# A coarse column shift inside the score matmul, coefficients shared between VectorE and GpSimd, and gates in two F32R passes

## The chip, the cores and the metric

The kernel runs on 1 core of a Trainium2 chip. The metric is device microseconds of one execution; a run of the kernel before takes 1344.95 us in the median of three (1344.68 to 1345.1). PE is TensorE, DVE is VectorE, ACT is ScalarE, POOL is GpSimd, and SP is the engine whose queue issues most of the DMAs.

## The reference

One transformer layer on x of 16 batches, 512 positions and 128 features: an attention and a feed-forward network (FFN), each on a layer-normed input, each layer-normed again and added. A head has 8 features (16 heads), a query is its own key, and every position has one of 64 buckets per head.

```python
scores = jnp.einsum('bhsd,bhtd->bhst', q, q) / jnp.sqrt(jnp.float32(E))
same = (b_hs[:, :, :, None] == b_hs[:, :, None, :]).astype(scores.dtype)
attn = jax.nn.softmax(scores * (NB - 2 + same), axis=-1)      # NB = 64
...
h = silu(tlin(x, w1_w, w1_s)) * tlin(x, w2_w, w2_s)           # tlin: x @ w.T * s, w of -1, 0, 1
h = gelu(tlin(h, h1_w, h1_s)); h = gelu(tlin(h, h2_w, h2_s))  # 512 wide
return tlin(h, w3_w, w3_s)
```

Scores times 62 or 63 make large exponents, so something has to be subtracted ahead of the exponential. All is in fp32.

## The kernel before

The program is straight-line code. A small planner (class Order) builds it: the parts of the work are generators that ask for an engine with a cost, a rank and what they wait for, and the planner's own clock decides the order in which each engine gets its instructions. On the chip every engine runs its list in that order. Buffers are named and handed out by pools (`logit_bufs`, `score_banks`, `ffn_banks`, `banks` and so on). Lower rank goes first: score matmuls have 0, attention 1, FFN 4.

*Batch preparation* (`prep`). The layer norm of x is applied by ACT with statistics that ACT sums ahead of time (`inputs`, L553 and L563). PE projects the queries (L635), which are split into three bf16 parts and written to DRAM. Buckets come from PE and go to DRAM too.

*Scores* (`gather`, `scores`). For each of 256 heads SP loads the parts back as 72 rows for the left and 72 for the right operand, nine products of parts and 8 features; one bf16 matmul of 128 x 512 per tile (L872), four tiles a head. A third load puts the head's bucket row on all partitions (bb).

*Coefficients* (`coeffs`, L890). DVE compares bb, kept as three rows of 172, with the bucket of the partition and adds 62.

*Logits* (`logits`, L925). DVE multiplies coefficient and score and keeps the row maximum of the tile. Scores are symmetric, so row maxima are column maxima.

*Shift and exponential* (`maxima`, `softmax`). Two heads' maxima are transposed by DVE (L958), written to DRAM (md), read back as one row on all partitions (mb, 256 KB), and POOL subtracts it from four tiles at once (L982). ACT takes the exponential (L987). Five heads of the first two batches go another way (`softmax_by_rows`).

*Weighted sum* (`attend`). For each group of four heads PE multiplies with the values (L1048); the result is copied, transposed, and divided by DVE (L1079, L1080). A logit buffer is held from its first tile to the group's product; there are 11.

*FFN* (`residual`, `added`, `ffn`). After the norms, PE makes the w1 and w2 gates in fp32 (L1200, eight matmuls a batch), ACT silu, DVE the product (L1170); two hidden layers (L1244, gelu L1258), and the output (L1282). The mean is taken out in the weights, not in the input. The FFN of batch b waits for the first hidden layer of batch b - 1; batch 15 goes in halves. POOL has the power -0.5 of the variances (L457). Dummy matmuls (`activity`, L1419) fill PE until the first FFN.

Of the kernel before, what the change touches and what calls it, by code (L numbers as in the profile page):

```python
# [14 lines left out]
BF16 = mybir.dt.bfloat16  # L15
AF = mybir.ActivationFunctionType
# [5 lines left out]
P = 128  # L22
EPS = 1e-5
NBKT = 64

# [165 lines left out]
def tile_lsh_attention_ffn(  # L191
    ctx: ExitStack,
    tc: tile.TileContext,
    x: bass.AP,
# [30 lines left out]
    KS = NP * NP * DH  # L225
    BR, BC, BP = 3, 172, 174
# [9 lines left out]
    LB = 11  # L236
    BY_ROWS = (3, 7, 11, 15, 19)
    SLOTS = H * NT
    N = B * SLOTS

# [39 lines left out]

    junk = const.tile([P, E], BF16, name="junk")
# [7 lines left out]

    block = const.tile([E, H], F32, name="block")  # L290
    nc.vector.reduce_sum(
        block, ident.rearrange("r (h d) -> r h d", d=DH), axis=AX.X
    )
    hp_sb = const.tile([E, H, NH], F32, name="hp_sb")
# [68 lines left out]
    score_banks = Pool("s", 3)  # L363
    ffn_banks = Pool("f", 3)
    banks = Pool("b", 2)
    logit_bufs = Pool("l", LB)
    row_bufs = Pool("r", 4)
    co_bufs = Pool("co", 4)
    mx_bufs = Pool("mx", 2)
    mb_bufs = Pool("mb", 3)  # L370
    row_mx_bufs = Pool("rx", 2)
    h_bufs = Pool("h", 3)
    x1_bufs = Pool("x1_", 2)
    xnt_bufs = Pool("xntf", 1)
    avs_bufs = Pool("avs", 1)
    a_bufs = Pool("a", 2)

    NB_ = B * NG
    gathered, exped = events(B * H), events(B * H)
    scored, weighed = events(N), events(N)  # L380
# [116 lines left out]
    def turned(xn, xnt, k, tp, tiles):  # L497

        cols = slice(tiles[0] * P, (tiles[-1] + 1) * P)

        def turn():
            for t in tiles:
                nc.tensor.transpose(tp[:, ts(t, P)], xn[:, t, :], ident)

        yield pe(0.125 * len(tiles), 2, turn)
        yield act(0.13 + 0.0925 * len(tiles), -2, lambda: nc.scalar.copy(xnt[:, cols], tp[:, cols]))
        od.put(banks, k)
# [21 lines left out]
    rs_x = const.tile([P, B, NT], F32, name="rs_x")  # L529
    nm_x = const.tile([P, B, NT], F32, name="nm_x")  # L530
    known = events(B)

    def inputs():
        for b0, b1 in zip(GROUPS, GROUPS[1:]):
            n = b1 - b0
            sums = const.tile([P, 2, n, NT], F32, name=f"sx_{b0}")
            ve = const.tile([P, n, NT], F32, name=f"vx_{b0}")
            late = 6 if b0 == 1 else LATE
            if b0 > 1:
                yield wait(gathered[1])  # L540
            for b in range(b0, b1):
                xt = p2.tile([P, NT, E], F32, tag="xtm", name=f"xtm_{b}", bufs=1)
                yield dma(
                    256,
                    2,
                    lambda: nc.sync.dma_start(
                        out=xt, in_=x[b].rearrange("(p t) e -> p t e", t=NT)
                    ),
                )

                def sum_(ts_):
                    for t in ts_:
                        nc.scalar.activation(  # L553
                            junk,
                            xt[:, t, :],
                            AF.Identity,
                            scale=ROOT / E,
                            accum_out=sums[:, 0, b - b0, t : t + 1],
                        )

                def square(ts_):
                    for t in ts_:
                        nc.scalar.activation(  # L563
                            junk,
                            xt[:, t, :],
                            AF.Square,
                            scale=-ROOT,
                            bias=sums[:, 0, b - b0, t : t + 1],
                            accum_out=sums[:, 1, b - b0, t : t + 1],
                        )  # L570

                yield act(1.0, late, lambda: sum_((0, 1)))
                yield act(1.0, late, lambda: sum_((2, 3)))
                yield act(1.2, late, lambda: square((0, 1)))
                yield act(1.2, late, lambda: square((2, 3)))
            yield act(
                0.22,
                -5,
                lambda: nc.scalar.activation(ve, sums[:, 1], AF.Identity, bias=eps),
            )  # L580
            yield pool(
                1.0,
                0,
                lambda: nc.gpsimd.tensor_tensor(
                    rs_x[:, b0:b1], ve, mhalf[:, 0:n], op=ALU.pow
                ),
            )
            k = yield get(banks)
            mp = bank(k, f"mp_{b0}")[:, 0 : n * NT].rearrange("p (b t) -> p b t", t=NT)
            yield act(0.22, -5, lambda: nc.scalar.copy(mp, sums[:, 0]))  # L590
            yield dve(
                0.1,
                1,
                lambda: nc.vector.scalar_tensor_tensor(
                    nm_x[:, b0:b1], mp, -(float(E) ** 0.5), rs_x[:, b0:b1], op0=ALU.mult, op1=ALU.mult
                ),
            )
            od.put(banks, k)
            for b in range(b0, b1):
                od.set(known[b])  # L600


    qds, bkds, bjs = {}, {}, {}

    def prep(b):
# [14 lines left out]
        if b:  # L620
            yield wait(known[b])
            xn = p2.tile([P, NT, E], F32, tag="xna", name=f"xn_a{b}", bufs=1)
            xnt = p1.tile([P, S], F32, tag="xnta", name=f"xnt_a{b}")
            yield from rescale(xt, lambda t: xn[:, t, :], (nm_x[:, b], rs_x[:, b]), ALL)
            k = yield get(banks)
            yield from turned(xn, xnt, k, bank(k, f"tp_a{b}"), ALL)
        else:
            xnt = p1.tile([P, S], F32, tag="xnta", name=f"xnt_a{b}")
            yield from norm_transposed(xt, xnt, f"a{b}", 1, ALL)
# [13 lines left out]
        qd = [  # L643
            dram.tile([H, DH, NP, S], BF16, tag="qd0", name=f"qd0_{b}"),
            dram.tile([H, NP, DH, S], BF16, tag="qd1", name=f"qd1_{b}"),
        ]
        kept = events(NP)

        def keep(i):
            def emit():  # L650
                nc.sync.dma_start(out=qd[0][:, :, i, :], in_=qparts[i])
                nc.sync.dma_start(out=qd[1][:, i, :, :], in_=qparts[i])

            yield dma(256, 1, emit, cost=0.7)
            od.set(kept[i])
# [97 lines left out]
        od.spawn(keep(0))  # L753
        yield wait(read)
# [57 lines left out]
    def gather(j, tag):  # L812
        b, h = divmod(j, H)
        yield wait(prepared[b])
        ql = p1.tile([KS, S], BF16, tag=f"ql{tag}", name=f"ql_{j}")
        qr = p1.tile([KS, S], BF16, tag=f"qr{tag}", name=f"qr_{j}")
        bb = p1.tile([P, BR * BP], BF16, tag=f"bb{tag}", name=f"bb_{j}")
        rows[j] = (ql, qr, bb, tag)

        yield dma(  # L820
            74,
            1 + j * 1e-3,
            lambda: nc.sync.dma_start(
                out=ql,
                in_=qds[b][1][h]
                .rearrange("i d s -> (i d) s")
                .unsqueeze(1)
                .to_broadcast([NP * DH, NP, S]),
            ),
            held=False,  # L830
# [658 lines left out]
```

## Time and profile before

| | |
|---|---|
| median of the runs | 1344.95 us |
| span of the profiled execution | 1343.1 us |
| PE, DVE busy | 1293.6 us (96%), 1220.4 us (91%) |
| ACT, POOL busy | 1119.6 us (83%), 1196.7 us (89%) |
| mean granted TensorE clock | 0.987 |
| DMA | 174.03 MB, 130 GB/s over the span |

The span goes from the first to the last instruction. A row of a group names line, engine, operation, output and inputs with their shapes, the count, busy microseconds in total, the mean nanoseconds of one, the idle time of the engine ahead of it and what ended that. An fp32 matmul has two records. Instructions of one engine overlap at their ends, so the sum of durations is more than busy time. In the view by stretch, each engine has its busy time and its number of instructions, and the clock and the share of DMA stand last.

### The profile page before, as it was taken

The page shows a single profiled execution, that of the slowest core. Times are in us where ns is not written, and L with a number is a line of the kernel's source. Part 1 is how long each engine was busy: PE and PEld are TensorE (multiplying, and loading weights), DVE is VectorE, ACT ScalarE, POOL GpSimd, SP SyncE. Part 2 cuts the span into 40 slices and gives each one's busy share as a digit, 9 for nine tenths or more (in the row PEclk, how much of TensorE's full clock was granted, in tenths as well). Part 3 has the DMA queues.
Part 4 walks back from the last instruction along what each step waited for, and adds up shares of the span by engine and source line. Part 5 has one row for each costly group of instructions (what it writes and reads, how often), then busy time and mean ns, then how long its engine had stood idle before and what let it go on. Part 6 is the DMA issues. An engine that isn't in the chain of part 4 may idle for free.

```text
span 1343.1 us, 21064 instructions
## 1 busy us (share of the span) xinstructions
PE 1293.6 (96%) x6009; PEld 577.7 (43%) x6009; DVE 1220.4 (91%) x3867; ACT 1119.6 (83%) x1560; POOL 1196.7 (89%) x316
## 2 busy tenths in 40 slices
PE   8999999998999999999999999999999999999897
PEld 3444344344443343444334344434444344434367
DVE  5999999999999899999999999999999999999220
ACT  3688888889998897988888788888989798888953
POOL 1497999999999999999999999999999999999810
PEclk9999999998999999999999999999999999999999
DMA  4755455455544445455544545454545545444100
GB/s 132 198 142 149 128 156 134 139 144 146 148 142 116 129 141 145 133 141 137 149 123 122 146 132 155 123 143 120 149 129 142 138 139 140 131 120 119 48 9 8
DMA packets 158865, 174.03 MB, mean 130 GB/s; under 512 B 33821, under 2 KB 117277, under 8 KB 158749
## 3 DMA queue, kind: packets, MB, share of 16 engines
q1 hardware_dynamic: 155937, 169.20, 45.7%
q10 hardware_dynamic: 2811, 3.48, 0.9%
q8 instruction: 48, 0.79, 0.2%
q14 instruction: 69, 0.56, 0.2%
HBM read 153.50 MB, written 19.13 MB: 129 GB/s over the span
## 4 chain that ended last, share of the span: by engine, by line
PE 55%; DVE 25%; DMA 7%; POOL 5%; issue 5%; ACT 3%; SPq 1%; POOLq 0%; ACTq 0%; DVEq 0%
PE hp L1244 23%; PE av L1048 12%; DVE l L925 12%; PE sp L872 10%; DVE co L890 9%; POOL l L982 5%; PE w L1200 4%; DMA mb<-md 4%; PE yp L1282 2%; PE op L1069 1%; DMA bb<-bkd 1%; DVE h L1170 1%; DMA ql<-qd 1%; ACT l L987 1%; PE pp L674 1%
## 5 line engine op out<-in xcount | busy, mean ns | idle before, releaser
L982 POOL TENSOR_TENSOR l<-l,mb 128x2048 f32<-128x2048 f32 x251 | 1134.9, 4553 | 39.8 <-DMA mb<-md 33.1
L925 DVE CUSTOM_DVE_ANT_0 l<-co,sp 128x512 f32<-128x512 bf16 x1024 | 663.0, 678 | 14.9 <-PE sp L872 10.0
L987 ACT ACTIVATE l<-l 128x2048 f32<-128x2048 f32 x251 | 478.2, 1908 | 38.9 <-POOL l L982 33.9
L1244 PE MATMUL hp<-h,h 128*128 128x512 f32 (+1 forms) x1088 | 495.5, 569 | 0.4 <-ACT h L1258 0.4
L890 DVE TENSOR_SCALAR co<-bb,bj 128x516 bf16<-128x516 bf16 x1024 | 450.1, 470 | 1.1 <-DMA bb<-bkd 0.7
L872 PE MATMUL sp<-qr,ql 72*128 72x512 bf16 x1024 | 346.6, 383 | 33.8 <-DVE mxpad L925 30.3
L1244 PEld LDWEIGHTS hp<-h,h 128*128 128x128 f32 x1088 | 202.0, 190 | 159.4 <-issue 134.7
L1048 PE MATMUL av<-l,vaug 128*32 128x512 f32 x2008 | 251.4, 607 | 0.0
L872 PEld LDWEIGHTS <-ql 72*128 72x128 bf16 x1024 | 91.2, 98 | 279.0 <-issue 258.4
L1200 PE MATMUL w<-xnt_f,w 128*128 128x512 f32 (+1 forms) x272 | 133.6, 591 | 4.4 <-ACT a L1188 4.2
L1048 PEld LDWEIGHTS av<-l,vaug 128*32 128x32 f32 x2008 | 55.1, 110 | 146.6 <-issue 123.2
L987 ACT ACT_TABLE_LOAD x87 | 111.6, 1283 | 1.5
L1419 PE MATMUL activity<-still 128*128 128x512 bf16 x325 | 89.5, 387 | 1.0 <-DVE still L283 1.0
L925 DVE DVE_READ_ACCUMULATOR2_ANT mxpad<- 128x1 f32 x1004 | 81.6, 81 | 0.0
L1258 ACT ACT_TABLE_LOAD x59 | 75.7, 1283 | 0.9
L1200 PEld LDWEIGHTS w<-xnt_f,w 128*128 128x128 f32 x272 | 51.5, 197 | 49.0 <-issue 23.8
L1062 ACT COPY avs<-av 128x512 f32<-128x512 f32 x64 | 37.0, 578 | 41.8 <-PE av L1048 41.6
L1170 DVE TENSOR_TENSOR h<-w,a 128x512 f32<-128x512 f32 (+1 forms) x68 | 44.1, 652 | 30.0 <-PE w L1200 19.6
L1282 PEld LDWEIGHTS yp<-w,h 128*128 128x128 f32 x512 | 65.4, 191 | 13.0 <-issue 9.0
L1282 PE MATMUL yp<-w,h 128*128 128x128 f32 x512 | 65.9, 275 | 0.0
L457 POOL TENSOR_TENSOR rs_y<-ve_y,mhalf 128x4 f32<-128x4 f32 (+1 forms) x17 | 16.5, 969 | 50.3 <-ACT ve_y L446 50.1
L1258 ACT ACTIVATE h<-hp,h1s 128x512 f32<-128x512 f32 (+1 forms) x68 | 42.0, 660 | 14.3 <-PE hp L1244 13.9
(105 smaller groups left out, 954.6 us busy)
## 6 DMA issues: line engine op xcount, KB each, us to landing
mb<-md SPq DMA_DIRECT2D x251, 256.0 KB
bb<-bkd SPq DMA_DIRECT2D x256, 130.5 KB
ql<-qd SPq DMA_DIRECT2D x256, 72.0 KB
qr<-qd SPq DMA_DIRECT2D x255, 72.0 KB
qd<-q SPq DMA_DIRECT2D x96, 128.0 KB
xta<-in_L_attn_x_dram SPq DMA_DIRECT2D x16, 256.0 KB
xtr<-in_L_attn_x_dram SPq DMA_DIRECT2D x16, 256.0 KB
xtm<-in_L_attn_x_dram SPq DMA_DIRECT2D x15, 256.0 KB
```

Of the source, the lines that this page charges most:

```text
L872: nc.tensor.matmul(sp, lhsT=ql[:, ts(t, P)], rhs=qr, start=True, stop=True)
L890: nc.vector.tensor_scalar(co, bb.rearrange("p (r c) -> p r c", c=BP)[:, :, 0:BC], bjs[b][:, c : c + 1], float(NBKT - 2), op0=ALU.is_equal, ...
L925: nc.vector.tensor_tensor_reduce(out=l, in0=co[:, 0:S], in1=sp, scale=1.0, scalar=-3.0e38, op0=ALU.mult, op1=ALU.max, accum_out=mx[:, t : ...
L982: lambda: nc.gpsimd.tensor_tensor(l, l, mb.unsqueeze(1).to_broadcast([P, NT, S]), op=ALU.subtract),
L987: yield act(1.82, 0, lambda: nc.scalar.activation(l, l, AF.Exp, scale=SCALE), "exp")
L1048: nc.tensor.matmul(av[k * Q : (k + 1) * Q, :], lhsT=va[:, t, c : c + Q], rhs=ls[gg * GH + k][0][:, t, :], start=(t == 0), stop=(t == NT - 1),)
L1170: lambda: nc.vector.tensor_tensor(h[:, c, cols], g2, a, op=ALU.mult),
L1200: lambda: nc.tensor.matmul(gp, lhsT=w_sb[which][:, 0, ts(c, P)], rhs=xnt[:, cols], start=True, stop=True),
L1244: lambda i=i: nc.tensor.matmul(hp, lhsT=w[:, i, ts(c, P)], rhs=hin[:, i, cols], start=(i == 0), stop=(i == NC - 1),),
L1258: nc.scalar.activation(h[:, c, cols], hp, AF.Gelu, scale=sc[:, c : c + 1])
L1282: nc.tensor.matmul(yp[:, ts(t, E)], lhsT=h[:, i, ts(t, P)], rhs=w_sb["w3"][:, i, :], start=(i == 0), stop=(i == NC - 1),)
L1419: nc.tensor.matmul(bk, lhsT=still, rhs=still.unsqueeze(1).to_broadcast([P, NT, P]), start=start, stop=stop,)
```

## The change

*Column shift.* In batches 1 to 15, no maximum is taken. A level, the rounded |q|^2/7.75 up to 4, times 0.125, stands for the column. 64 rows are appended to each operand of the score matmul: on the left a one-hot of the bucket (1 where the position's bucket is the row's number), on the right (one-hot - 63) times the column's level. Their product adds (same - 63) x level to the score, and the coefficient 62 + same makes that -3906 x level whether the buckets agree or not. The exponential then takes a constant bias of -25. The query part has 64 rows in place of 72 (it drops one of the nine products of parts), so the matmul has 128 rows. Batch 0 keeps the old way, in two halves a head.

*Coefficients.* In batches 1 to 15, heads 1, 3, 5 and so on have theirs from POOL. The bucket row is now four rows of 128.

*Gates.* w1 and w2 are kept as plain -1, 0, 1 in F32R; the FFN input, with its mean subtracted, is split into a rounded F32R part and the rest, and each gate is two matmuls that add up in PSUM. The scale of w2 goes into the product on DVE.

*Around it.* Statistics of x are taken by DVE per batch instead of ACT ahead of time; row buffers 6 for 4, logit buffers 7 for 11, mb buffers 2 for 3; FFN and small PSUM pools are one of five banks. A verdict checks that all reciprocal denominators lie between 1e-34 and 1e26 and that the F32R weights equal the loaded ones; if not, the whole old body, which stands behind it in the program, is run as well.

```diff
+    CHAIN = (2, 2, 1, 1, 0, 1, 2, 0, 0, 2)
+    KS = (len(CHAIN) - 1) * DH
-    BR, BC, BP = 3, 172, 174
+    BR, BC, BP = 4, 128, 130
...
 def coeffs(heads, bufs, pooled):
+    (nc.gpsimd if pooled else nc.vector).tensor_scalar(
         co, bb.rearrange("p (r c) -> p r c", c=BP)[:, :, 0:BC], bjs[b][:, c : c + 1],
         float(NBKT - 2), op0=ALU.is_equal, op1=ALU.add)
...
 def logits(heads):
+    if mx is None:
+        nc.vector.tensor_tensor(l[:, t, :], co, sp, op=ALU.mult)
+        return
...
+def weights_of(j, l):
+    nc.scalar.activation(l, l, AF.Exp, bias=base, scale=SCALE)
+def levels(b, square):
+    nc.tensor.matmul(rowp, lhsT=own, rhs=square, start=True, stop=True)
+    nc.vector.tensor_scalar(rowp, rowp, LEVELS, WHOLE, op0=ALU.min, op1=ALU.add)
+    nc.vector.tensor_scalar(level, rowp, -WHOLE, UNIT, op0=ALU.add, op1=ALU.mult)
+    nc.sync.dma_start(out=zds[b], in_=level)
+def code(b, h, kp):                     # two heads on 128 partitions
+    nc.sync.dma_start(out=pb, in_=bkds[b][two]...)      # 130 KB
+    nc.sync.dma_start(out=pz, in_=zds[b][two]...)       # 128 KB
+    nc.gpsimd.tensor_scalar(hot[:, 0, :]..., pb..., number, None, op0=ALU.is_equal)
+    nc.vector.scalar_tensor_tensor(
+        hot[:, 1, :], hot[:, 0, :], 1.0 - NBKT, pz, op0=ALU.add, op1=ALU.mult)
+# in gather, per head:
+    nc.sync.dma_start(out=qlr[NBKT:P], in_=code[i * NBKT : (i + 1) * NBKT])
+def bounded(rd):                        # per group of four heads
+    for limit, op in ((LEAST, ALU.is_gt), (MOST, ALU.is_lt)):
+        nc.vector.scalar_tensor_tensor(sound, rd, limit, sound, op0=op, op1=ALU.mult)
...
 def gate(which, c, gp):
+    for i, r in enumerate(xnt):         # rounded part, rest: both F32R
+        nc.tensor.matmul(gp, lhsT=w_sb[which][:, 0, ts(c, P)], rhs=r[:, cols],
+                         start=i == 0, stop=i == 1)
 def product(c, g2, kb, half):
-    nc.vector.tensor_tensor(h[:, c, cols], g2, a, op=ALU.mult)
+    nc.vector.scalar_tensor_tensor(h[:, c, cols], g2, w_sb["gs"][:, c : c + 1], a,
+                                   op0=ALU.mult, op1=ALU.mult)
...
+def tile_lsh_attention_ffn(tc, *args):
+    nc = tc.nc
+    with tc.tile_pool(name="verdict", bufs=1) as kept:
+        doubt = kept.tile([1, 1], I32, name="doubt")
+        body(tc, doubt, *args)
+        v = nc.values_load(doubt, min_val=0, max_val=2**20)
+    with tc.If(v > 0):
+        body(tc, None, *args)
```

## The prediction

> **What bounds the kernel now.** I read the busy time by stretch first, because the stages have different limits. I cut the span where DVE starts the first logit tile of batch 1 (97.5 us) and where it has done the last one of batch 15 (1247).
>
> ```profile
> core 0: us, PE busy (x) PEld busy (x) DVE busy (x) ACT busy (x) POOL busy (x), PEclk, DMA share, GB/s
> 0.00:97.50 97.50, 92.74 (x456) 41.97 (x457) 79.24 (x251) 59.62 (x144) 47.99 (x22) 1.00 0.57 160
> 97.50:1247.00 1149.50, 1116.04 (x5180) 480.82 (x5178) 1128.12 (x3575) 1004.61 (x1315) 1120.35 (x283) 0.99 0.50 136
> 1247.00:1343.10 96.10, 84.86 (x374) 54.87 (x374) 13.08 (x43) 55.35 (x102) 28.39 (x13) 0.97 0.06 20
> ```
>
> In the middle stretch (fifteen batches, 76.6 us each) DVE and POOL are both busy 97 to 98%. The last stretch is PE alone, finishing the feed-forward work. Then the groups, for who holds those engines:
>
> ```profile
> L982 POOL TENSOR_TENSOR l<-l,mb 128x2048 f32<-128x2048 f32 x251 | 1134.9, 4553 | 39.8 <-DMA mb<-md 33.1
> L925 DVE CUSTOM_DVE_ANT_0 l<-co,sp 128x512 f32<-128x512 bf16 x1024 | 663.0, 678 | 14.9 <-PE sp L872 10.0
> L890 DVE TENSOR_SCALAR co<-bb,bj 128x516 bf16<-128x516 bf16 x1024 | 450.1, 470 | 1.1 <-DMA bb<-bkd 0.7
> L1200 PE MATMUL w<-xnt_f,w 128*128 128x512 f32 (+1 forms) x272 | 133.6, 591 | 4.4 <-ACT a L1188 4.2
> L1362 POOL TENSOR_TENSOR w<-w,scale 128x512 f32<-128x512 f32 x2 | 2.5, 1268 | 15.3 <-DMA scale<-in_L_ffn_w_s_dram 15.3
> ```
>
> POOL is full of one thing, the subtraction (L982): 16 x 4.53 + 3 x 0.97 (L457) = 75.4 us a batch. DVE's durations overlap, so a sum needs the pace from start to start, which the order of time gives:
>
> ```profile
> 52.41 0.86 DVE L890 TENSOR_SCALAR co<-bb,bj 128x516 bf16<-128x516 bf16 x2
> 53.19 0.67 DVE L925 CUSTOM_DVE_ANT_0 l<-co,sp 128x512 f32<-128x512 bf16 x1
> 53.79 0.08 DVE L925 DVE_READ_ACCUMULATOR2_ANT mxpad<- 128x1 f32 x1
> 53.79 0.68 DVE L925 CUSTOM_DVE_ANT_0 l<-co,sp 128x512 f32<-128x512 bf16 x1
> ```
>
> Two coefficients take 0.78 (0.39 each), a logit tile 0.60 to 0.61. In the same way: tensor_tensor from PSUM 0.60 (L793), scalar_tensor_tensor 0.65 (L758), tensor_scalar from PSUM 0.67 (L686), bn_stats 0.22, aggregate 0.09, one-column tensor_scalar 0.14, transpose 0.13. With these the middle's DVE instructions sum to 1137 of 1149.5 us. PE likewise: a 512-column bf16 score 0.215, an fp32 one 0.43 per record and 0.86 per matmul (two records).
>
> ```profile
> 642.15 0.38 PE L872 MATMUL sp<-qr,ql 72*128 72x512 bf16 x1
> 642.36 1.02 PE L1200 MATMUL w<-xnt_f,w 128*128 128x512 f32 x2
> 643.22 0.38 PE L872 MATMUL sp<-qr,ql 72*128 72x512 bf16 x1
> ```
>
> By these PE's middle work is 1071 us, so 78 us are gaps. The chain of waits (PE 55%, DVE 25%, POOL 5%) wanders between engines that are all nearly full. **POOL and DVE bound the middle, 1% apart; PE is 6% behind them and alone bounds the end.** Taking POOL's load away therefore gains only as far as DVE also gets lighter.
>
> **The change, part by part**, in the span of the profiled execution (1343.1; the median of the runs shown is 1344.95, 1.85 above it). Counts are from the order of the built program's instructions.
>
> *Subtraction gone (L982; 239 heads of batches 1 to 15 in it).* 1083 us off POOL. Alone it gives nothing while DVE stays at 1137. With it go 119 transposes on DVE (x 0.13 = -15.5), the md/mb round trip, and 239 x 256 KB of DMA. In its place come, per pair of heads, two loads, a one-hot on POOL, a code on DVE, and two 128 KB copies into the score operands. DMA ends near today's 174 MB at half load, and SP issues 1159 transfers instead of 1329: no cost.
>
> *Logit tile as a plain tensor_tensor.* 0.61 to 0.60 on 959 tiles: -9.6.
>
> *Coefficients of every second head to POOL.* 481 fewer on DVE x 0.39 = -187.6. POOL gets 476 of these and 117 one-hots. No POOL row has this form: below, a 128x128 memset at 0.20; above, the 128x512 two-input multiply at 1.27 (L1362). From 128x512 at 1.27 and 128x2048 at 4.53 a POOL element costs 2.1 ns plus 0.18 fixed; the one-input select on 128x128 took 0.295, so 0.9 ns an element and 0.64 for 512. I take 0.64: 593 x 0.64 and 60 x 0.97 (L457) = 438 us. Even 1.27 gives 811, and POOL would bind only from 1.72. Hidden by DVE's work on the other head.
>
> *DVE's 544 remaining coefficients* now read four rows of 128 instead of three of 172. The row is 0.39; if the even rows halved what exceeds the 0.14 of a one-column instruction it would be 0.265; above, waiting out one POOL instruction, 1.03. I take 0.39, the only row of that kind.
>
> *New on DVE, middle:* 117 codes with two SBUF inputs, 128x512; bounds 0.39 and 0.65, taken 0.60: +70. Levels, 28 x 0.67: +19. Range marks, 118 x 0.12 (a 96x16 one lasts 0.17 and overlaps): +14. Statistics of x moved from ACT, and a mean subtracted ahead of the FFN: +30 (48 stats, 48 aggregates, 108 one-column). The low half of the FFN input, 14 x 0.60: +8. Gate products with a scale, 56 x 0.05: +3.
>
> Sum on DVE in the middle: -15.5 - 9.6 - 187.6 + 70 + 19 + 14 + 30 + 8 + 3 = **-69**, 1137 to 1068. With the same idle 12 us: 1149.5 to about 1080, 72 us a batch.
>
> *Gates in two F32R passes.* 8 matmuls of 0.86 a batch become 16. Bounds per pass: 0.215 (bf16 row) and 0.86 (fp32 row). One pass can only pay if it is one record, so I take 0.215: 6.9 to 3.4 us a batch. PE's middle work is then 1005 (by the program's order), 75 us below DVE's 1080: the saving is hidden, except at the end.
>
> *Waits added.* A code on DVE waits for POOL's one-hot and two loads; behind it stand logit tiles. The copy on SP waits for the code; behind it stand later heads' loads. Six row buffers (were four) put both some 20 us ahead of the scores, against 2 to 4 us for a load. ACT loses 65 us of sums and 12 table loads and gains 15 squares: never the bound.
>
> *Head.* DVE gets 8 us more work before batch 1 and has 18 idle there: +6.
>
> *End.* The order says what the diff does not: on PE, after the last score, 84.2 us of work are left before, 94.5 after. FFN b's gates come after b + 1.9 batches of scores now, after b + 2.0 to 2.3 in the changed program, so 19 hidden-layer products of batch 13 are left too. PE is packed there: +10.
>
> *Verdict and branch.* The sums are ready before FFN 14. Each engine loads one number and jumps over the second body; as long as one small load (2.98 us for the first of the trace): +3, between 0 and 10.
>
> Total: -69 + 6 + 10 + 3 = -50. Span 1293, time **1296**.
>
> **A rule against the trace.** The 1024 coefficients of the trace lasted 0.432 to 0.492 us whether POOL was idle or not, and the 251 subtractions 4.500 to 4.649 with DVE full and with DVE idle after 1247: no sign that the two engines hinder each other. The Trainium skill (SBUF — State Buffer, Who interferes with whom) says that they do, the second to start waiting to the end of the first, when the DVE instruction reads by two ports or has two SBUF inputs. The skill's VectorE: DVE Perf Modes (What auto-detection actually checks) lets a 16-bit one-source instruction use two ports, at twice the rate again, when the outer counts of both sides are even. By these pages three rows kept the old coefficients out of that mode and four rows let the new ones in: by 4 elements a cycle my estimate from the page is 0.25 each, -67 us, with the waits of the second rival on top. No run so far shows either.
>
> **Rivals.**
> *1. PE takes over.* If coefficients cost 0.265, DVE's middle loses 60 more, to 1020, under PE's 1005 plus gaps. With half of today's 78 us of gaps the middle is 1044: 36 below the forecast, **1260**. For: PE is 92% full already. Against: no row for 0.265.
> *2. DVE and POOL block each other* (the slower side). 476 coefficients, 117 codes and 118 marks, 711 in all, would now collide. POOL is busy 438 of 1080 us, 41%; half an instruction left is 0.32; a mean wait of 0.13 makes 711 x 0.13 = +92: **1388**. It decides against the change from 49/711 = 0.07 us a piece. For: codes and marks have two SBUF inputs, a kind which the trace does not have beside a busy POOL. Against: the durations above.
> *3. F32R is not one pass.* At 0.43 gates cost as now; PE's middle 1053, and with 60 us of gaps 1113: **1333**. At 0.86, about 1390.
> *4. Stalls on seven logit buffers* (were eleven). A group of four fills in 17 us and leaves some 8 later; seven last 29 at 4.2 a head. If every group lost 0.4 us, 60 x 0.4 = +24: **1320**.
> *5. It doesn't do what it says:* the verdict comes out positive and the whole old body runs as well, near **2640**. The reciprocal denominators have to lie between 1e-34 and 1e26; worked out from the inputs with the shift, they lie between 2e-13 and 2e20, and -1, 0 and 1 survive any rounding, so I hold it unlikely.
>
> **How the numbers follow.** Forecast (1275 to 1320) 50%, rival 1 15%, rival 2 15%, rival 3 9%, rival 4 8%, rival 5 or a POOL price above 1.72 3%. 1255 to 1345 leaves out most of rival 2, the far end of 3, and 5: about 18%. A measurement of this kernel can tell about 0.2% (2.7 us). Faster by more: 50 + 15 + 8 + 5 of rival 3's + 2 of rival 2's (short waits) = 80%; within, 1.5 of each of these two = 3%; slower, the other 11.5 of rival 2, 2.5 of rival 3 and the last 3 = 17%.
>
> **What would show it.** Right: POOL well under 60% busy, DVE about 98% in the middle, coefficients near 0.39 to 0.47 on DVE, no subtraction on POOL after batch 0, gate records 0.215 apart, PE busy for some 105 us after the last score. Wrong: coefficient durations on DVE with a wide spread (rival 2), DVE idle on score matmuls (rival 1), PE waiting for logit buffers, or a second copy of the body in the trace.

## The result: a quarter slower, and the profile after

The changed kernel takes **1670.37 us** (median of four runs, 1669.89 to 1673.07) against 1345.03 for the kernel before: ratio 1.242, 95% interval [1.2405, 1.2442]. The prediction (1296, faster) has the wrong sign and its range misses. The profiled execution took 1670.38 us, span 1668.5. The first view is the stretches: head, batches 1 to 15 (first to last logit tile), end.

```profile
core 0: us, PE busy (x) PEld busy (x) DVE busy (x) ACT busy (x) POOL busy (x), PEclk, DMA share, GB/s
0.00:135.50 135.50, 114.16 (x544) 49.60 (x545) 107.71 (x290) 47.56 (x73) 69.58 (x46) 0.94 0.47 129
135.50:1562.60 1427.10, 1157.54 (x5095) 493.59 (x5093) 1077.84 (x2493) 994.58 (x1131) 1197.11 (x651) 0.92 0.42 107
1562.60:1668.50 105.90, 94.89 (x417) 63.13 (x415) 18.12 (x67) 56.03 (x120) 7.20 (x9) 0.97 0.04 11
```

Against before: head +38, middle +277.6 (95.1 us a batch instead of 76.6), end +9.8; together the 325.4 that the span grew. In the middle no engine is full: POOL 84%, PE 81%, DVE 76%. DVE is busy for even less time than before (1078 us against 1128). The granted clock fell from 0.99 to 0.92. The groups say what changed hands (lines left out are marked ...):

```profile
L914 POOL TENSOR_SCALAR co<-bb,bj 128x512 bf16<-128x512 bf16 x480 | 962.0, 2019 | 192.4 <-issue 155.0
L962 DVE TENSOR_TENSOR l<-co,sp 128x512 f32<-128x512 bf16 x960 | 618.4, 677 | 75.4 <-PE sp L888 34.7
...
L888 PE MATMUL sp<-qlr 128*128 128x512 bf16 (+1 forms) x1024 | 380.6, 405 | 275.8 <-DVE l L962 239.7
...
L1086 DVE SCALAR_TENSOR_TENSOR hot<-hot,pz 128x512 bf16<-128x512 bf16 x120 | 98.3, 820 | 238.3 <-POOL hot L1074 196.7
```

A coefficient (L914) lasts 2.02 us on POOL, three times what I took; a one-hot (L1074) lasts 1.57. With 32 coefficients, 8 one-hots and 4 powers POOL has 64.6 + 12.6 + 4 = 81 us of work a batch, over 4 more than the whole batch took before. And everybody waits for somebody: PE's scores for DVE (239.7 us), DVE's codes (L1086) for POOL's one-hot (196.7). In order of time, POOL, DVE, and PE's next scores:

```profile
799.72 6.00 POOL L914 TENSOR_SCALAR co<-bb,bj 128x512 bf16<-128x512 bf16 x3 [1.48 <-issue]
805.70 1.56 POOL L1074 TENSOR_SCALAR hot<-pb,number 128x512 bf16<-128x512 bf16 x1
807.30 1.17 DVE L1086 SCALAR_TENSOR_TENSOR hot<-hot,pz 128x512 bf16<-128x512 bf16 x1 [3.62 <-POOL hot L1074]
809.12 1.18 PE L888 MATMUL sp<-qlr 128*128 128x512 bf16 x2 [3.71 <-DVE l L962]
```

POOL does three coefficients ahead of the one-hot, and DVE stands 3.62 us at the code. Logit tiles whose scores are made stand behind it, since PE in turn waits 3.71 us until DVE takes the next one.

### The profile page after: what moved, and what is told of

Same layout as the page of the kernel before. It is cut to its first block, busy times and chain, and to the rows that moved or that the text cites. A ratio compares the mean times of both kernels' runs of the same rounds, so it can differ in the third digit from the quotient of the medians.

```text
span 1668.5 us, 20345 instructions
## 1 busy us (share of the span) xinstructions
PE 1366.6 (82%) x6052; PEld 606.3 (36%) x6052; DVE 1203.7 (72%) x2848; ACT 1098.2 (66%) x1322; POOL 1273.9 (76%) x706
## 5 line engine op out<-in xcount | busy, mean ns | idle before, releaser
L914 POOL TENSOR_SCALAR co<-bb,bj 128x512 bf16<-128x512 bf16 x480 | 962.0, 2019 | 192.4 <-issue 155.0
L962 DVE TENSOR_TENSOR l<-co,sp 128x512 f32<-128x512 bf16 x960 | 618.4, 677 | 75.4 <-PE sp L888 34.7
L1007 ACT ACTIVATE l<-l,base 128x2048 f32<-128x2048 f32 x240 | 479.3, 2001 | 195.5 <-DVE l L962 194.5
L888 PE MATMUL sp<-qlr 128*128 128x512 bf16 (+1 forms) x1024 | 380.6, 405 | 275.8 <-DVE l L962 239.7
L1505 PE MATMUL hp<-h,h 128*128 128x512 f32 (+1 forms) x1088 | 530.8, 598 | 0.5 <-DVE vaug L804 0.2
L1086 DVE SCALAR_TENSOR_TENSOR hot<-hot,pz 128x512 bf16<-128x512 bf16 x120 | 98.3, 820 | 238.3 <-POOL hot L1074 196.7
L888 PEld LDWEIGHTS <-qlr 128*128 128x128 bf16 (+1 forms) x1024 | 96.4, 101 | 407.6 <-issue 369.1
L914 DVE TENSOR_SCALAR co<-bb,bj 128x512 bf16<-128x512 bf16 x544 | 243.4, 478 | 0.6 <-DMA bb<-bkd 0.6
L1074 POOL TENSOR_SCALAR hot<-pb,number 128x512 bf16<-128x512 bf16 x120 | 188.4, 1570 | 15.5 <-DMA pb<-bkd 12.7
L1130 POOL TENSOR_TENSOR l<-l,mb 128x1024 f32<-128x1024 f32 x24 | 57.0, 2398 | 25.0 <-DVE co L914 12.5
```

What stands on the lines that cost most here:

```text
L888: nc.tensor.matmul(sp, lhsT=qlr[:, 0, ts(t, P)], rhs=qlr[:, 1, :], start=True, stop=True,)
L914: (nc.gpsimd if pooled else nc.vector).tensor_scalar(co, bb.rearrange("p (r c) -> p r c", c=BP)[:, :, 0:BC], bjs[b][:, c : c + 1], float(N ...
L962: nc.vector.tensor_tensor(l[:, t, :], co, sp, op=ALU.mult)
L1007: 1.82, 0, lambda: nc.scalar.activation(l, l, AF.Exp, bias=base, scale=SCALE), "exp"
L1074: (nc.gpsimd if HOT == "pool" else nc.vector).tensor_scalar(hot[:, 0, :].rearrange("p (r c) -> p r c", c=BC), pb.rearrange("p (r c) -> p r ...
L1086: lambda: nc.vector.scalar_tensor_tensor(hot[:, 1, :], hot[:, 0, :], 1.0 - NBKT, pz, op0=ALU.add, op1=ALU.mult),
```

## The experiments

Theories, as the expectations name them: A, the price of POOL's compares; B, DVE and POOL blocking each other; C, in e1 and e2 the shift itself with its longer way into the score operands and seven logit buffers, from e6 on too few PSUM banks between PE and DVE, in which PE leaves scores for DVE; D, the loads that a code waits for; E, half clock after PE's waits; F, an order planned for wrong durations. "Idle" and "work" of DVE per batch are added up from the trace between the first logit tiles of batches 4 and 12, a duration ending where the next instruction starts; a duration that another engine stretched counts as work. Time at half clock follows from the mean granted clock c: the records have only 1.0 and 0.5, so it is 2 (1 - c) x span. In the edits shown here, constants that stand on lines of their own are put on one line.

| | us | ratio, interval | DVE work, idle a batch | us at half clock |
|---|---|---|---|---|
| before | 1345 | | 76.0, 1.8 | 35 |
| after | 1670.4 | 1.242 [1.2405, 1.2442] | 72.2, 24.0 | 254 |
| one-hots on DVE (e1) | 1506.2 | 1.119 [1.1135, 1.1248] | 74.3, 12.1 | 147 |
| coefficients on DVE (e2) | 1564.7 | 1.163 [1.1561, 1.1691] | 78.0, 13.0 | 197 |
| both on DVE (e5) | 1571.1 | 1.168 [1.1652, 1.1716] | 79.1, 12.5 | 213 |
| POOL's costs right in the plan (e3) | 1628.4 | 1.210 [1.2040, 1.2158] | 74.1, 21.7 | 280 |
| e5, loads early (e6) | 1514.7 | 1.126 [1.1218, 1.1306] | 78.8, 7.3 | 136 |
| e6, a quarter of the heads on POOL (e9) | 1506.9 | 1.121 [1.1178, 1.1235] | 77.4, 7.2 | 163 |
| e6, DVE's costs right (e10) | 1517.1 | 1.128 [1.1249, 1.1304] | 78.7, 11.0 | 185 |
| e10, half of the heads on POOL (e11) | 1524.9 | 1.135 [1.1317, 1.1374] | 74.7, 13.1 | 180 |
| e10, banks 4 and 4 (e12) | 1526.2 | 1.134 [1.1314, 1.1375] | 78.5, 11.5 | 177 |
| e11, fitting figures (e14) | 1484.6 | 1.104 [1.1020, 1.1057] | 74.5, 9.5 | 122 |
| e14, a load counts 2.6 (e15) | 1504.5 | 1.120 [1.1177, 1.1215] | 74.0, 10.0 | 114 |
| e14, three rows (e17) | 1471.2 | 1.092 [1.0880, 1.0959] | 76.1, 8.0 | 109 |
| e14, codes later (e18) | 1513.5 | 1.126 [1.1243, 1.1283] | 73.6, 12.1 | 145 |
| e14, both (e19) | 1494.6 | 1.112 [1.1098, 1.1135] | 75.8, 9.1 | 119 |

### What a compare costs on POOL (e4)

```diff
+for i in range(8): pool.tensor_scalar(h, four, bj, 62.0, op0=ALU.is_equal, op1=ALU.add)  # L43
+for i in range(8): pool.tensor_scalar(h, four, bj, None, op0=ALU.is_equal)               # L47
+for i in range(8): pool.tensor_scalar(h, flat, bj, 62.0, op0=ALU.mult, op1=ALU.add)      # L53
...
+for i in range(24): vec.tensor_scalar(d, four, gate2, 62.0, op0=ALU.is_equal, op1=ALU.add)   # L79, POOL subtracts
+for i in range(24): vec.tensor_scalar(d, three, gate2, 62.0, op0=ALU.is_equal, op1=ALU.add)  # L81, POOL subtracts
+for i in range(24): vec.tensor_scalar(d, four, gate5, 62.0, op0=ALU.is_equal, op1=ALU.add)   # L90, POOL compares
```

> Not the layer: single instructions of 128x512, eight of a kind, on an idle chip; the output is zeros. On POOL alone: the coefficient as it is (four rows, two operations, scalar from SBUF), on one flat run, with one operation, with a constant instead of the scalar from SBUF, in f32, with multiply and add, with multiply alone, a bf16 two-input multiply, a bf16 copy, an f32 two-input subtraction, and 256 elements. If 2.0 us is the form's own price: 2.0 for the first, 1.57 with one operation, and half of the part above 0.2 for 256 elements; if it is the rows or the bf16, the flat or the f32 one is near the 1.27 of the two-input f32 subtraction; if comparing costs, multiply and add is near 1.2. Then DVE's coefficient with four rows and with three, alone (0.26 and 0.39 apart), beside POOL's subtraction and beside POOL's coefficients: if two engines block each other only in the four-row form, four rows last up to one POOL instruction (1.3 and 2.0) and three rows stay at 0.39 to 0.47.

The groups of that run (busy us, mean ns):

```profile
L43 POOL TENSOR_SCALAR h<-bb,bj 128x512 bf16<-128x512 bf16 x8 | 15.8, 1996 | 0.7 <-DVE h L36 0.7
L47 POOL TENSOR_SCALAR h<-bb,bj 128x512 bf16<-128x512 bf16 x8 | 12.3, 1564 | 0.0
L53 POOL TENSOR_SCALAR h<-bb,bj 128x512 bf16<-128x512 bf16 x8 | 5.4, 700 | 0.0
L61 POOL TENSOR_TENSOR g<-bf,g 128x512 f32<-128x512 f32 x8 | 10.1, 1263 | 0.5
L79 DVE TENSOR_SCALAR d<-bb,gate 128x512 bf16<-128x512 bf16 x24 | 31.1, 1371 | 0.0
L81 DVE TENSOR_SCALAR d<-b,gate 128x516 bf16<-128x516 bf16 x24 | 9.4, 468 | 0.0
L90 DVE TENSOR_SCALAR d<-bb,gate 128x512 bf16<-128x512 bf16 x24 | 9.9, 490 | 0.0
```

On POOL it is the operation that costs. Compare and add takes 2.0 us whether the row is flat, in four rows, fp32 or compared with a constant (1.93 to 2.00); a compare alone 1.56, a multiplication alone 1.57; multiply and add, over the same 512 elements, 0.70, and the two-input subtraction 1.26. So the bound of 1.27 from a two-input row was no bound. Comparing as such is not the reason, since a multiplication alone costs as much; why one pair of operations is cheap and the other dear stays open. On DVE alone the four-row form comes every 0.27 us and the three-row form every 0.40. Beside POOL's subtraction the four-row form comes every 31.1/24 = 1.30 us, one POOL instruction apiece; three rows are not touched (0.39).

The profile before had a warning of this. A power over 40 elements a partition took 169 ns an element there, where I worked with 0.9 to 2.1:

```profile
L584 POOL TENSOR_TENSOR rs_x<-vx,mhalf 128x40 f32<-128x40 f32 x1 | 6.7, 6745 | 0.0
```

### The four rows by themselves (e16)

```diff
-    BR, BC, BP = 3, 172, 174      # the kernel before, nothing else
+    BR, BC, BP = 4, 128, 130
```

> The kernel before with bucket rows of 4 x 128 in place of 3 x 172, nothing else. By rival 2 of the prediction (DVE and POOL block each other): POOL subtracts 97% of the middle, 4.5 us apiece, so most coefficients on DVE wait for an end of a subtraction, durations spread from 0.34 to 4.6 us, and the time is far above 1345, 1600 or more. If the four-row form is only faster: coefficients 0.27 us apart, and 1345 or a little less, since POOL stays full.

2238.6 us (one run) from that one line. A group of this run, and its DVE and POOL in order of time:

```profile
L890 DVE TENSOR_SCALAR co<-bb,bj 128x512 bf16<-128x512 bf16 x1024 | 1212.2, 1213 | 1.6 <-DMA bb<-bkd 1.1
```

```profile
595.95 4.62 DVE L890 TENSOR_SCALAR co<-bb,bj 128x512 bf16<-128x512 bf16 x1
600.48 0.67 DVE L925 CUSTOM_DVE_ANT_0 l<-co,sp 128x512 f32<-128x512 bf16 x1
```

```profile
595.76 9.15 POOL L982 TENSOR_TENSOR l<-l,mb 128x2048 f32<-128x2048 f32 x2
```

The coefficient that starts at 595.95 is running when POOL's first subtraction of the two ends (595.76 + 4.55 = 600.31), and ends 0.26 us later, at 600.57: that is the 0.27 us of its work after the subtraction. A quarter of the coefficients (247 of 1024) last over 0.6 us; I had expected most of them to. Rival 2 is real in the form that the change introduced, and the trace of before could not show it, as its three rows never met it. In the changed kernel the partner is a compare, which holds DVE less (L90): its coefficients take 11.8 us a batch for 32, 0.37 each against 0.27 unblocked, and codes 0.71 against 0.61 in e5. That is 32 x 0.10 + 8 x 0.10 = 4 us a batch, 60 us of work.

### POOL's load away (e1, e2, e5)

```diff
-HOT = "pool"                                # e1 and e5
+HOT = "dve"
-HEADS_C = tuple(range(1,16,2))              # e2 and e5
+HEADS_C = ()
```

> The changed kernel with the one-hot of each pair of heads on DVE instead of POOL; the coefficients of every second head stay on POOL. Theory A (POOL's price and its queue: a coefficient of 2.0 us, and DVE's codes standing behind one-hots that POOL reaches only after four of them): POOL needs 32 x 2.0 + 4 x 1.0 = 68 us a batch in place of 81, the 197 us that DVE waited for one-hots are gone, the pace falls from 95 us a batch to 80 to 85: 1440 to 1520 us. Theory B (the two engines block each other): DVE's instructions stay long and POOL still has 64 us of coefficients beside them, 1600 us or more. Theory C (the shift itself, with its longer way into the score operands and seven logit buffers): no change, 1670.

> The changed kernel with all coefficients on DVE; POOL keeps the one-hots (8 x 1.57 us a batch). DVE then has 64 x 0.60 of logits, 64 x 0.27 of coefficients, 5 of codes and 17 of the rest, 77 to 79 us a batch. Theory A: DVE bounds, 106 + 15 x 78.5 + 108, about 1390 us. Theory B: the same, as POOL is nearly idle, and DVE's coefficients keep within 0.31 to 0.35 us but for a few. Theory C: DVE still waits for the score matmuls and the time stays over 1550.

> One-hots and all coefficients on DVE; POOL keeps only its powers and the work of batch 0. Theory A (POOL's slow compares and what they couple are the whole loss): with both gone the time is near 1400 or below, POOL under 15% busy. Theory D (what remains is the chain of a code: two loads, one-hot, code on DVE, copy, score; the loads come about 7 us after their issue where the planner counts on 2.6 plus 0.8, and DVE stands in order behind a code that waits): 1470 to 1530, with 70 to 120 us of DVE idle ahead of codes and one-hots that end with a load, as in the two runs before.

The one-hots are worth 164 us, the coefficients 106, and both together only 99: once the one-hots are on DVE, taking the coefficients off POOL as well makes the kernel 65 us slower (e1 to e5). So A is a large part, but it is not all: with POOL 8% busy the time is still 1571, above both cases of the expectation, and e2 missed A's 1390. B does not explain e1, which came out far below its 1600. DVE then has 79.1 us of work a batch, 3 more than before (the coefficients save 7.8 and the transposes 1.1; codes cost 4.9, one-hots 2.1, levels 1.2, range marks 1.1, the rest is statistics and the low half), and stands idle for 12.5. Who is waited for in e2:

```profile
DVE hot L1086 <- DMA pz<-zd: 68.8, 45, 3.0
DVE l L962 <- PE sp L888: 49.6, 64, 2.2
```

DVE stands at codes whose second load (pz) has not come, and then at scores that PE made late.

### The order and the buffers (e3, e6, e9 to e12)

```diff
-yield pool(0.55, RCO, emit) if pooled else dve(0.39, 4, emit)     # e3; the one-hot 1.57
+yield pool(2.0, RCO, emit) if pooled else dve(0.3, 4, emit)
-NPB, NR, LBF, DMA_LAT = 2, 6, 7, 2.6                              # e6, on e5
+NPB, NR, LBF, DMA_LAT = 4, 8, 8, 7.0
-HEADS_C = ()                                                      # e9, on e6; POOL counted 2.0
+HEADS_C = (3, 7, 11, 15)                                          # NPB 3, NR 7
-dve(0.39, ...)                                                    # e10, on e6; e11: HEADS_C 1, 3, 5 ..., NPB 3, NR 7
+dve(0.27, ...)
-NS, NF = 3, 5                                                     # e12, on e10
+NS, NF = 4, 4
```

> The changed kernel with the same work on the same engines; only the planner is told what the instructions took (coefficient on POOL 2.0 in place of 0.55, one-hot 1.57, coefficient on DVE 0.3 in place of 0.39), so that the order of each engine's list changes. Theory A, if the order made for 0.55 is what costs: POOL's 81 us a batch bounds, 120 + 15 x 83 + 108, 1450 to 1500 us. If POOL's work alone matters and the order does not: 1620 to 1670. Theory B: as now, within 2%.

> As the run with all on DVE, and in addition the loads are made earlier: the planner counts 7.0 us for a load instead of 2.6, four pair buffers instead of two, eight row buffers instead of six, eight logit buffers instead of seven. Same instructions. Theory D: DVE's idle time ahead of codes and one-hots falls below 30 us, and the time falls by 70 or more against that run, to 1370 to 1430. Theory C (the score banks, three in PSUM, and the order of PE and DVE are what holds it): the time falls by less than 30, DVE goes on waiting for scores and PE for logit tiles.

> As the run with early loads, but coefficients of every fourth head on POOL, which the planner counts at their measured 2.0 us (seven row buffers and three pair buffers, for room). POOL gets 16 x 2.0 = 32 us a batch, DVE loses 16 x 0.27 = 4.3 a batch, 65 in all. If a share that fits POOL's pace helps: 30 to 60 below the run with early loads. If a DVE operation that waits for POOL's end costs as much as it saves (240 collisions at up to 2 us, or POOL's order waiting for DVE's): within 20 of it, or above.

> As the run with early loads (all on DVE), but the planner counts a coefficient and a one-hot on DVE at their measured pace, 0.27 us, instead of 0.39: its plan was one in which DVE has 87 us of work a batch where the trace has 78.8. Same instructions. Theory F (the order is a plan for costs that are wrong, and PE and DVE then run into each other): idle time of DVE falls from 7.4 us a batch to under 4, and the time to 1440 to 1480. Theory E (a PE wait of about 1 us is followed by 3.4 to 10 us at half the granted clock, which makes the next waits, whatever the plan): within 20 of that run's 1515.

> As the run with the planner's costs right, but coefficients of every second head on POOL again at 2.0 us (planner's count too), one-hots on DVE, seven row and three pair buffers. POOL has 64 + 4 = 68 us a batch, DVE 78.8 - 8.6 = 70.2 and what POOL blocks. If DVE's work is what is left to bind: 60 to 120 below the run with the right costs, 1340 to 1420. If the waits between the three engines bind: 1450 or more, with POOL waiting for logit tiles and PE for DVE.

> As the run with the planner's costs right, but four score banks and four of the others in PSUM instead of three and five. Theory C (PE stalls since the third score bank is not yet read by DVE): PE's waits for logit tiles fall by more than half and the time by 30 or more. Otherwise within 15, or slower since the feed-forward work has fewer banks.

With 81 us on POOL a right plan helps little (e3, 42 us; within 1620 to 1670, the case in which the order does not matter). Earlier loads, together with more buffers, help by 56 (e6). DVE's wait for pz in e5 and in e6 (us, times, longest):

```profile
DVE hot L1086 <- DMA pz<-zd: 103.7, 73, 3.5
DVE hot L1086 <- DMA pz<-zd: 31.5, 19, 3.6
```

The wait falls by 72 us, nearly to D's 30, but the time by less than D's 70. Theory F as I put it fails: with DVE's costs right the time stays (e10), as E had it. Moving coefficients back to POOL gains 8 (e9; the intervals meet), or takes work from DVE and returns it as idle time (e11: 74.7 and 13.1). A fourth score bank leaves PE's wait for logit tiles at 120.9 us against 122.3 (e10) and the time 9 us higher, so C's banks are not it.

### Without the code (e7)

```diff
+depth = KS - DH if j // H in running else KS     # no loads, one-hots, codes, copies
+nc.scalar.activation(l, l, AF.Exp, bias=base, scale=SCALE * 1.0e-3)
```

> As the run with all on DVE, but the code chain is left out: no pair loads, one-hots, codes or copies; scores are made from the 64 query rows alone, without the column shift, and the exponential is scaled by 1/1000 so that its sums stay in range; so this is not the layer. DVE loses 120 one-hots at about 0.3 and 120 codes at 0.6, some 110 us of work. Theory D: the time falls by these 110 and by the 70 to 120 us of waits as well, to 1290 to 1340. Theory C: it falls by the work alone or less, to 1390 or more, and PE still waits over 100 us for logit tiles.

1510.5, and it says nothing on D. DVE's work fell to 72.6 us a batch, but PE became the bound: 773 of 800 us busy between 300 and 1100. About half of its fp32 records of the hidden layers came 533 ns apart (193 of 377 in that stretch), nearly all others 429 as in the kernel before (where 12 of 421 were that slow), at a granted clock of 1.0 in the records. I have no cause for that; on PE only the data of the softmax and the depth of the score matmul differ from e5, where 429 was the rule. The run is no floor.

### Waits of PE and its clock (e13)

```diff
+for gap in (1, 2, 3, 5, 8):
+    for _ in range(5):
+        for k in range(gap): vec.tensor_copy(r[(n + 1) % 2], acc[n % 2])
+        n += 1; block(64)
```

> Not the layer, output zeros: blocks of 64 bf16 matmuls of 128x512, and between two blocks PE waits for one, two, three, five or eight copies out of PSUM by DVE, five times each. Theory E: after a wait of 1 us or more the granted clock is 0.5 for one 3.4 us window or more, so that the next block's first matmuls are 0.43 apart instead of 0.215; the longer the wait the surer. If the clock has nothing to do with PE's waits, all blocks run at 0.215.

One stretch for each gap (idle time ahead of a block, from the starts of PE's records: 0.95, 1.7, 2.4, 3.8, 6.0 us; one run):

```profile
core 0: us, PE busy (x) PEld busy (x) DVE busy (x) POOL busy (x), PEclk, DMA share, GB/s
17.00:77.00 60.00, 56.71 (x260) 25.27 (x259) 2.90 (x5) 0.00 (x0) 1.00 0.00 1
92.00:155.00 63.00, 55.89 (x256) 25.01 (x256) 6.54 (x10) 0.00 (x0) 1.00 0.00 1
170.00:237.00 67.00, 57.58 (x256) 25.40 (x256) 8.75 (x14) 0.00 (x0) 0.97 0.00 0
257.00:335.00 78.00, 63.22 (x257) 26.83 (x257) 13.83 (x21) 0.00 (x0) 0.88 0.00 1
357.00:446.00 89.00, 65.20 (x256) 27.20 (x256) 22.48 (x33) 0.00 (x0) 0.85 0.00 0
```

E holds, at a longer wait than I expected: single waits of 0.95 and 1.7 us never lowered the clock (column PEclk), those of 2.4 sometimes, longer ones nearly always, for one or two periods of 3.41 us. The Trainium skill (TensorE: Matmul & The Clock Gate, Part 1: The HAM clock gate) says that a gate looks at free-running windows of 3413 ns and halves the clock after an idle one; the records agree in length, but here waits shorter than a window were enough. In the changed kernel PE ran 254 us at half clock instead of 35: 127 us of PE's time lost instead of 18. That waits can cause it is shown by this run; that it lengthens them in turn is argued. Over the other runs it goes with DVE's idle time only roughly (e9 has 7.2 us and 163, e15 has 10.0 and 114), and how much of the 1670 us it costs is not shown.

### Fitting figures, three rows, later codes (e14, e15, e17, e18, e19)

```diff
-NPB, NR, LBF, DMA_LAT = 3, 7, 8, 7.0                               # e14, on e11
+NPB, NR, LBF, DMA_LAT = 3, 8, 7, 4.0                               # a coefficient on DVE counts 0.34
-DMA_LAT = 4.0                                                      # e15
+DMA_LAT = 2.6
-BR, BC, BP = 4, 128, 130                                           # e17
+BR, BC, BP = 3, 172, 174
+yield ("rest", 4.0)                                                # e18, ahead of the one-hot; NPB = 5
```

> Half of the coefficients on POOL, one-hots on DVE, and a plan whose figures come from the traces: 2.0 us for a coefficient on POOL, 0.34 for one on DVE beside it, 4.0 us for a load, eight row buffers, three pair buffers, seven logit buffers. DVE's work is about 74 us a batch, POOL's 68. If the order was at fault: DVE's idle time falls from 13 us a batch to under 5 and the time to 1330 to 1420. If waits between engines, each followed by half-clock stretches of PE, come whatever the order: 1480 to 1530 as the runs so far.

> As the run before it, but a load counts 2.6 us in the plan, as in both kernels. If the 7.0 us of the earlier runs was what spoiled their order, this one is as good as the run with 4.0 or better; if loads really come late for this plan, codes wait again 40 us and more and the time is 30 above it.

> As the run with fitting figures (1485), with bucket rows of 3 x 172 for coefficients and one-hots on both engines, counted at 0.39 on DVE. If the blocking of DVE by POOL spoils the order: durations on DVE narrow again (0.43 to 0.50), POOL's coefficients 1.99 to 2.1, and the time falls by 40 or more. If the late loads do it: DVE still waits 60 us and more for them, and the time stays within 20, since 0.39 is also what the four-row form took beside POOL.

> As the run with fitting figures, but each code is planned 4 us later after its loads, with five pair buffers instead of three. If the late loads hold the rest: DVE's idle time ahead of codes falls from 69 us (in 800) to under 20 and the time by 40 or more, to 1440 or less. If not, the wait moves to scores and the time stays within 20.

> Both edits. If the two causes are separate and both real, the gains add: 1380 or less, and at best the kernel before's 1345, since DVE's work is 75 us a batch in either. If one hides the other: about as the better of the two.

A plan with a load at 4.0 us is the best with four rows (1484.6; 2.6 gives 1504.5, and 7.0 with slightly other buffers and costs gave 1524.9), so the order counts for some 20 to 40 us, not for the 70 and more that theory F needs. Three rows take another 13 (0.9%; the intervals do not meet) and make DVE's durations narrow again, as this line view of e17 shows (min/median/max ns; after had 307/347/2454):

```profile
L914 DVE TENSOR_SCALAR co<-bb,bj x544: 439/473/483, 24.5 to 1394.1; 128x516 bf16<-128x516 bf16 x182
```

Later codes make it 29 us slower, outside both cases of e18: the wait moves, and PE waits for the copied code.

```profile
PE sp L888 <- DVE l L962: 66.9, 91, 5.6
PE sp L888 <- DMA qlr<-hot: 52.9, 14, 8.2
```

Both edits (e19, 1494.6) come out between the two, so the gains do not add.

What stays in e17, the best version, are above all waits for pz, 96.5 us over the span. But this wait alone does not set the time. In e11 and then in e14, which is 40 us faster:

```profile
DVE hot L1086 <- DMA pz<-zd: 23.4, 18, 3.4
DVE l L962 <- PE sp L888: 113.5, 122, 4.1
DVE hot L1086 <- DMA pz<-zd: 112.7, 75, 3.5
DVE l L962 <- PE sp L888: 16.3, 21, 2.1
```

The idle time moves between the code and the scores, and less of it at one place is not yet less time. Why the loads are late shows in DMA's share, in e17 between two waits (1 us a row; SP had issued two pairs of pb and pz from 780.3 on, its copy at 787.2 took until 790.4, and only then came other loads):

```profile
787.00:788.00 1.00, 1.00 (x11) 0.25 (x3) 1.00 (x4) 0.39 (x2) 1.00 (x1) 1.00 0.14 47
788.00:789.00 1.00, 1.00 (x6) 0.62 (x4) 1.00 (x2) 0.77 (x2) 1.00 (x2) 1.00 0.14 45
789.00:790.00 1.00, 1.00 (x6) 0.67 (x6) 1.00 (x3) 1.00 (x1) 1.00 (x1) 1.00 0.13 45
790.00:791.00 1.00, 1.00 (x5) 0.34 (x4) 1.00 (x3) 0.98 (x2) 1.00 (x2) 1.00 0.13 44
791.00:792.00 1.00, 0.01 (x1) 0.00 (x0) 1.00 (x2) 0.99 (x2) 1.00 (x1) 1.00 0.79 195
```

While only pair loads are in flight the share (next to last column) is 0.13 to 0.14: 0.135 x 16 = 2.2 engines of 16. The single packets of these four microseconds say the same: two are in flight for 3.35 us and three for 0.64. When other loads join, the share is 0.79. The Trainium skill (DMA: Bandwidth & Descriptors, Why a DMA increments its semaphore by 16 and not by 1) says that a load is spread over the largest number of engines up to 16 that divides the slowest dimension of both sides; the pair loads read [2, 64, row], which makes two. At 45 GB/s a pair of loads, 130 + 128 KB, takes 5.9 us, and all eight pairs of a batch take 47 us at this rate. In e2 a pb issued at 774.15 let POOL's one-hot start at 781.06, 6.9 us later. That the width of two is the cause of the late loads is argued from these rows and the page: no run with the dimension the other way round was made, and it is open what it would give.

## Why the prediction was wrong, step by step

- POOL's load away *"gains only as far as DVE also gets lighter"*, and the sum on DVE: right in total. I had 1068 us for the middle; 72.2 a batch make 1083. Logit tiles, statistics and the code (0.61 unblocked) came out as summed, levels at 0.60 instead of 0.67. That coefficients took 0.37 where I took 0.39 is luck: unblocked they take 0.27, and POOL's blocking, which the sum left out, adds the other 0.10.
- *"Coefficients of every second head to POOL … I take 0.64"*, upper bound 1.27: **the first step that failed.** 2.02 us and 1.57 for a one-hot make 81 us a batch, above the point (1.72) from which I said POOL would bind. I took the price per element from other operations; e4 shows that on POOL the operation decides. I passed over the warning of the profile before, a power at 169 ns an element (L584, in the part on e4).
- *"Waits added"*, codes and copies *"some 20 us ahead of the scores, against 2 to 4 us for a load"*: **the second.** The loads of a pair take 6 to 7 us, and they are only the first step of a row that goes on over POOL, DVE and SP. Even in e5, without POOL, DVE idles 12.5 us a batch where I kept 0.8.
- *"With the same idle 12 us"*: the term that carries the error, and the two steps above are why. The sum of work was right within 2%; the idle time of the middle was not 12 us but about 24 x 15 = 360, and the middle took 1427 us instead of 1080. A sum of durations bounds the time only for an engine that nobody makes wait.
- *Rival 2*: its mechanism is real (e16), its size here about 4 us a batch, 60 us of work, against the 92 I gave it. The rule that I set against the trace held beside the subtraction (one POOL instruction apiece, e4), but not for the whole length of a compare. It is not what lost most: three rows gave 13 on top of e14 (e17).
- *Rival 1* (0.265): the pace was right, 0.27 unblocked; PE did not take over. *Rival 3* failed: a gate pass is one record, 0.23 us apart in a row, and a score matmul with the two passes behind it takes 0.68 us (0.215 + 2 x 0.23). *Rival 4*: not seen on its own. *Rival 5*: the second body was not run; its partner in the 3%, a POOL price over 1.72, was what happened.
- *Head +6*: measured +38, and 131 to 152 us before batch 1's logits in e5, e6, e14 and e17, so it is not POOL's load; it was not taken apart further. *End +10 and verdict +3*: +9.8 together, but in the other runs the end takes from 64 us (e3) to 95 (e15), so this agreement says little. The last line of the sum is off by one: 1293 and 1.85 make 1295, not 1296.

In e17, 133.3 us over before are left by the profiled spans: head 50.5, middle 100.5 (83.3 a batch; DVE 76.1 of work and 8.0 idle between batches 4 and 12), end -17.7. No version beat the kernel before. DVE's work is 72 to 79 us a batch in all of them against 76.0, so even without any idle time they had at most 4 us a batch to gain (8 in the changed kernel if the 4 us of blocking went too): what the shift puts on DVE (codes, one-hots, levels, marks) costs nearly what it and the faster coefficients save.

## What to carry to other kernels

Before moving an operation to an engine, time that operation there, in that form: over the same 512 elements two operators differed by a factor of three (0.70 and 2.0 us, e4). When two engines are full and in step, a new chain of load, compare, code, copy costs not its durations but the waits of engines that run their lists in order, and longer waits of PE (2.4 us and more in e13) can come back as half-clock time. A wait that goes away at one place can come back at another (e11 and e14), so judge an edit by the time and not by the wait. A change of layout that makes one instruction faster (0.40 to 0.27 us) can chain it to another engine: look at who else is busy before taking the faster form.

## What the runs showed of the hardware

- POOL, 128x512: compare and add 2.0 us, compare 1.56, multiply 1.57, multiply and add 0.70, copy 0.62.
- DVE, one-input bf16 compare: 0.27 us in four rows of 128, 0.40 in three of 172; beside POOL's two-input subtraction 1.30 and 0.39; beside POOL's compare 0.41 (9.9/24) and 0.39.
- PE's clock fell to half for 3.41 or 6.83 us after an idle time of 2.4 us (two of five times), 3.8 (four of five) and 6.0 (five of five), not after 0.95 or 1.7; and in e7 about half of its fp32 records came 533 ns apart instead of 429, with no sign in the granted clock.
- Loads whose source has an outermost dimension of two moved at 45 GB/s together, two packets at a time, with 0.135 of the DMA engines busy (e17).
- A pass of an F32R matmul over 512 columns, 128 deep: one record, 0.23 us (changed kernel).
